# A running account for late matmuls, z in the head's gaps, and a lower bound moved to GpSimd: an adaLN block with Mamba and hyper-connections

## The chip, the core and the metric

The kernel runs on one core of one Trainium2 chip. Its time is device microseconds (us) of one execution; a run's figure is the median of several. Five engines work side by side, each through its own queue in order: TensorE (PE; its weight loads are shown as PEld), VectorE (DVE), ScalarE (ACT), GpSimd (POOL) and SyncE (SP). Loads are issued from SyncE's queue, most stores from ScalarE's. An instruction that waits holds up all that stands behind it on its engine.

## The reference

The input x is 4 x 512 x 1024 in float32. Six modulation rows per batch element come from one product, and the two gates are bounded below in size:

```python
mod = (_silu(L0_c) @ L0_wmod).reshape(L0_c.shape[0], 6, 1, -1)
sa, ca, ga, sb, cb, gb = (mod[:, 0], mod[:, 1], mod[:, 2], mod[:, 3], mod[:, 4], mod[:, 5])
ga = (2 * (ga >= 0) - 1) * jnp.maximum(jnp.abs(ga), 0.25)
gb = (2 * (gb >= 0) - 1) * jnp.maximum(jnp.abs(gb), 0.25)
h = _layernorm(x, axis=-1) * (1 + ca) + sa
x = x + ga * attn(h)
h = _layernorm(x, axis=-1) * (1 + cb) + sb
x = x + gb * ffn(h)
```

`attn` is a Mamba block: h is projected to x and z (2048 channels each); x goes through a causal convolution of four taps and a silu to xc; xc is projected to dt, B and C (64 + 16 + 16 columns), each normalized; dt is projected back to 2048 channels and through a softplus; a scan over time runs for each channel and each of 16 states, `h = exp(dt * A) * h + dt * B * xc`, and its outputs are summed over the states with C; D * xc is added, the result is multiplied by silu(z) and projected to 1024 columns. `ffn` mixes four streams of 256 columns with matrices that come from 50 Sinkhorn iterations on logits of the normalized h.

## The kernel before, in words

Time is cut into eight blocks of 256 rows (k = 0 to 7, two for each batch element), and the 2048 channels into four quads of 512 (q = 0 to 3).

**Head** (up to line 1191; a scheduler puts its instructions into order): the modulation products SA and CA, layernorm and transpose of block 0, then the eight x products of block 0 (`product_x`, matmuls pp at L613). Their finish on ScalarE, VectorE (L629, the taps) and GpSimd (L641) yields xc. Then `product_bc` (px, L694), whose finish normalizes, transposes (pe, L739) and stores B and C, then `stage_dt(0, 0)` (pd L771, softplus L782, u L803, the transposes pa L821 and the copies acc L826), then the two halves of z's first quad (`product_z`, pz L661; sgz, sz L673 to L678), then the transposes of block 1 (`norm(1)`, copies ht L583).

**Loop** (order written out by hand): 8 x 64 steps, one for each block, quad and state. A step g has two scans on VectorE (L1157), each over half of the quad's channels; four exponentials for step g + 1 on ScalarE (L1122); the scan's input w for step g + 2 on GpSimd (L1108), in one of three buffers; on TensorE eight transposes hq (L1133) of step g - 1 into two PSUM tiles; and on VectorE two sums of them into acc (L1143). Between these, a step has six ticks. At each tick, side tasks that wait for a gap in VectorE or for a due time are taken up, and `paced` (L369) hands out matmuls of the projections for later blocks. The products stand in one queue: x of the next block (pp), z (pz), the output projection of the block before (po, L842), B and C of the next block (px), and in block 0 the modulation products GA, CB, SB and GB (L425, L470). A unit of the queue is one 128-row matmul into 256 columns, two records in the trace. `go_on(budget)` (L338) takes units until the budget in columns is spent or the product at the front must wait. Each block has a planned rate (columns by ticks); what is behind the plan is `debt`, and transposes that other tasks put on TensorE are taken off it (`aside`). Weights come through three buffers; a load is issued when its product is among the first three of the queue.

The output products of block k - 1 wait for the last quad's y, which is ready some steps into block k. In the last block, three quarters of its own output product are taken early and wait for y of the third quad.

`product_rows` (L464) makes the rows CB, SB and GB in quarters of 4 x 256. For GB the finish takes a gap in VectorE and calls `away_from_zero` (L411): L412 to L415, four instructions. Then ScalarE's queue stores the quarter (L485).

**Tail**: the last quad is gated on VectorE (L911), transposed (py, L926) and multiplied (po), added to x and stored; the last two tiles go through layernorm to the FFN's logits; the Sinkhorn iterations of the other tiles run on VectorE meanwhile (L187 to L216), and the mixing products and sums end the kernel.

Of the kernel before, what the change touches and what calls it, by code (L numbers as in the profile page):

```python
# [12 lines left out]
ALU = mybir.AluOpType  # L13
# [7 lines left out]
TB = 256  # L21
# [10 lines left out]
STEPS = NQ * N  # L32
TICKS = 6
LAG, TAP_LAG, ACT_LAG, POOL_LAG, DMA_LAG = 2, 3, 5, 10, 12
MAKE_UP = 1.3
TURN = 64
E = R + 2 * N
NS, C = 4, 256
# [18 lines left out]
def adaln_block(  # L57
# [22 lines left out]
    vec, act, pool, pe = nc.vector, nc.scalar, nc.gpsimd, nc.tensor  # L80
# [32 lines left out]
    ab = const.tile([P, 2, NTT, NS], F32, name="ab")  # L113
# [154 lines left out]
    with ExitStack() as ph:  # L268
# [15 lines left out]
        clock = [0]  # L284

        def route(g):
            got = next(g, None)
            if got == "v":
                gaps.append(g)
            elif got is not None:  # L290
                waiting.append((clock[0] + max(got, 1), g))

        def spawn(g):
            route(g)

        def take(what, idle=1):
            while not free[what]:
                yield idle
            free[what] -= 1

        def give(what):
            free[what] += 1
# [10 lines left out]
        def due():  # L313
            for _ in range(len(waiting)):
                at, g = waiting.popleft()
                if at <= clock[0]:
                    route(g)
                else:
                    waiting.append((at, g))

        def drain():
            while gaps or waiting:
                while gaps:
                    route(gaps.popleft())
                clock[0] += 1
                due()
# [6 lines left out]
        def ahead():  # L333
            while loaded[0] < min(3, len(queue)):
                queue[loaded[0]][1]()
                loaded[0] += 1

        def go_on(budget):  # L338

            spent = 0  # L340
            while queue and spent < budget:
                ahead()
                got = next(queue[0][0], None)
                if got is None:
                    queue.popleft()
                    loaded[0] -= 1
                elif got == 0:
                    break
                else:
                    spent += got  # L350
            return spent

        def whole():

            while queue:
                if not go_on(1):
                    while gaps:
                        route(gaps.popleft())
                    clock[0] += 1
                    due()  # L360
            drain()
# [6 lines left out]

        def paced(parts):  # L369

            debt = 0.0
            for columns, ticks in parts:
                rate = columns / ticks
                for _ in range(ticks):
                    debt += rate - owed[0]
                    owed[0] = 0
                    if debt > 0:
                        debt -= go_on(min(debt, MAKE_UP * rate))
                    yield

        def wload(key, src, shape=(P, HC, TB)):
            def load_it():
                w = p1.tile(list(shape), F32, name="w_" + "_".join(map(str, key)), tag="wts", bufs=3)
                load(w, src)
                weights[key] = w

            return load_it
# [11 lines left out]
        def bank(name, shape):  # L399
            return ps_mm.tile(list(shape), F32, name=name, tag="mm")  # L400
# [10 lines left out]
        def away_from_zero(m, sg, ab):  # L411
            vec.tensor_scalar(sg, m, 0.0, 2.0, ALU.is_ge, ALU.mult)  # L412
            vec.tensor_scalar(ab, m, -1.0, 0.25, ALU.mult, ALU.max)
            vec.tensor_tensor(ab, ab, m, ALU.max)
            vec.scalar_tensor_tensor(m, sg, -1.0, ab, ALU.add, ALU.mult)  # L415
# [48 lines left out]
        def product_rows(kind, q):  # L464

            yield from take("mm", 0)
            w = weights.pop(("mod", kind, q))
            pm = bank(f"pmr_{kind}_{q}", (B, TB))
            for k in range(HC):
                pe.matmul(pm, sc[:, k, :], w[:, k, :], start=(k == 0), stop=(k == HC - 1))  # L470
                yield TB

            def finish():
                yield LAG
                yield from take("row")
                mr = p1.tile([B, 3, TB], F32, name=f"mr_{kind}_{q}", tag="row", bufs=5)
                m, sg, ab = mr[:, 0, :], mr[:, 1, :], mr[:, 2, :]
                act.activation(m, pm, AF.Copy, bias=1.0 if kind == CB else 0.0)
                give("mm")
                yield ACT_LAG  # L480
                if kind == GB:
                    yield "v"
                    away_from_zero(m, sg, ab)
                    yield LAG
                store(row_dram[kind][:, q * TB : (q + 1) * TB], m)  # L485
                give("row")

            spawn(finish())
# [17 lines left out]
        def load_constants():  # L506
            load(cw, conv_w)
            load(cb, conv_b)
            load(lnw, ln_w.partition_broadcast(P))
            load(dtb, dt_bias)  # L510
            load(dtw, dtproj_w)
            load(dpar, d_param)
            load(aneg, a_log)
            act.activation(aneg, aneg, AF.Exp)
            vec.tensor_scalar(aneg, aneg, -1.0, None, ALU.mult)
# [131 lines left out]
        def product_z(k, q, s):  # L647

            if s == 0:
                yield from until(("h", k), 0)  # L650
                m = NQ * k + q
                if m >= 2:
                    yield from until(("gate", m - 2), 0)
                szs[k, q] = p1.tile([P, TT, 2, 2 * P], F32, name=f"sz_{k}_{q}", tag="sz", bufs=2)
            sz = szs[k, q]
            yield from take("mm", 0)
            w = weights.pop(("z", k, q, s))
            pz = bank(f"pz_{k}_{q}_{s}", (P, TT, 2 * P))
            for t in range(TT):
                for h in range(HC):  # L660
                    pe.matmul(  # L661
                        pz[:, t, :], hts[k][:, h, PAD + t * P : PAD + (t + 1) * P], w[:, h, :],
                        start=(h == 0), stop=(h == HC - 1),
                    )
                    yield TB
            if s == 1:
                done.add(("z", k, q))

            def finish():
                yield LAG  # L670
                yield from take("sgz")
                sg = p1.tile([P, TT, 2 * P], F32, name=f"sgz_{k}_{q}_{s}", tag="sgz")
                act.activation(sg, pz, AF.Tanh, scale=0.5)  # L673
                act.copy(sz[:, :, s, :], pz)
                give("mm")
                act.activation(sg, sg, AF.Copy, scale=0.5, bias=0.5)  # L676
                yield ACT_LAG
                pool.tensor_tensor(sz[:, :, s, :], sz[:, :, s, :], sg, ALU.mult)  # L678
                give("sgz")
                if s == 1:  # L680
                    done.add(("sz", k, q))

            spawn(finish())
# [339 lines left out]
        def add_x(k, lo, hi):  # L1023
            for p in range(lo, hi):
                queue.append((product_x(k, p), wload(("x", k, p), in_w[p])))

        def add_z(k, q):
            for s in range(2):
                queue.append((product_z(k, q, s), wload(("z", k, q, s), in_w[NP + 2 * q + s])))

        def add_bc(k):
            queue.append((product_bc(k), wload(("bc", k), xproj_w, (P, DC, E))))
# [147 lines left out]
        whole()  # L1180
        load_constants()
        add_x(0, 0, NP)
        add_bc(0)
        whole()
        spawn(stage_dt(0, 0))
        drain()
        add_z(0, 0)
        whole()
        spawn(norm(1))
        drain()  # L1190
# [2 lines left out]
        with tc.manual_schedule():  # L1193
# [5 lines left out]
            for k in range(NBLK):  # L1199
# [9 lines left out]
                for s in range(STEPS):  # L1209
                    g = k * STEPS + s  # L1210
                    q, n = divmod(s, N)
# [31 lines left out]
    with ExitStack() as ph:  # L1243
# [12 lines left out]
        for i in range(NTT):  # L1256
# [5 lines left out]
            k, r = divmod(i, TT)  # L1262
# [164 lines left out]
```

## Time and profile before

| what | us or share |
|---|---|
| median of three runs | 2542.53 (2541.72 to 2544.48) |
| profiled execution: its time, its span | 2546.19, 2544.4 |
| mean granted clock of TensorE | 0.963 |
| head, up to the first scan | 128.3 |
| loop, first scan to the last sum | 128.3 to 2308.0 |
| tail | 2308 to 2544 |

Times in the trace are microseconds from the span's start. Busy shares say how full an engine is; a line of a group names the source line, engine and operation, the output and inputs with their sizes, how many there were, busy time and mean duration (ns), and the idle time of the engine ahead of them with what ended most of it. Most of the working below goes by single stretches: a timeline gives start, duration, engine, line and operation, with the idle time ahead of it in brackets.

### The profile page before, as it was taken

Reading aid. Unit: us, or ns where it says so; the run is one execution under the profiler, and the core shown is the slowest. Engines: PE = TensorE matmul, PEld = TensorE weight load, DVE = VectorE, ACT = ScalarE, POOL = GpSimd, SP = SyncE. Lnnn points to the kernel's source line nnn. Section 1 sums busy time; section 2 is a strip of 40 time slices with the busy share of each in tenths; the row PEclk is TensorE's granted clock in tenths of the full one; section 3 lists DMA queues with packets and bytes.
Section 4 is the critical chain, followed back from the end, with each engine's and each line's share of the span. In section 5 each row is a group of like instructions: output and inputs, shape, how many; then the busy total and the mean of one; then the engine's idle time right before and its main releaser. Section 6 shows DMA issues by size and latency. Waiting matters only on the chain.

```text
span 2544.4 us, 38522 instructions
## 1 busy us (share of the span) xinstructions
PE 2351.9 (92%) x13224; PEld 1969.1 (77%) x13224; DVE 2286.8 (90%) x3539; ACT 1701.3 (67%) x3775; POOL 1803.9 (71%) x1199
## 2 busy tenths in 40 slices
PE   8899989999999999999999999999999999885578
PEld 5766577888888887888788878887888877774567
DVE  2289999999899998999899999999999989979988
ACT  2366567676867686767777786768676767752466
POOL 0257568777967697778877796779676888872395
PEclk9899989999999999999999999999999999987689
DMA  7433423334423343334333433343333422323802
GB/s 262 144 134 133 150 96 133 108 120 150 142 101 123 125 162 112 114 134 151 110 131 108 154 133 108 127 143 141 111 114 110 161 100 100 116 92 102 315 18 116
DMA packets 74339, 330.98 MB, mean 130 GB/s; under 512 B 8496, under 2 KB 25312, under 8 KB 47456
## 3 DMA queue, kind: packets, MB, share of 16 engines
q1 hardware_dynamic: 62784, 311.56, 34.5%
q10 hardware_dynamic: 11360, 16.96, 1.8%
q8 instruction: 106, 1.74, 0.3%
q14 instruction: 89, 0.73, 0.1%
HBM read 303.14 MB, written 25.35 MB: 129 GB/s over the span
## 4 chain that ended last, share of the span: by engine, by line
PE 37%; DVE 24%; ACT 10%; POOL 7%; issue 6%; DMA 2%; POOLq 0%; SPq 0%; DVEq 0%; ACTq 0%
DVE w L1157 11%; PE po L842 9%; PE hq L1133 8%; PE pz L661 7%; PE pp L613 7%; DVE acc L1143 5%; ACT da L1122 4%; POOL w L1108 3%; DVE xc L629 2%; DMA xr<-x_dram 2%; PE oa L1336 1%; POOL hh L976 1%; ACT dv L782 1%; ACT L1122 1%; ACT L782 1%
## 5 line engine op out<-in xcount | busy, mean ns | idle before, releaser
L1108 POOL TENSOR_TENSOR w<-u,b 128x1024 f32<-128x1024 f32 x512 | 1209.1, 2363 | 478.5 <-PE hq L1133 359.4
L1122 ACT ACTIVATE da<-dv,aneg 128x255 f32<-128x255 f32 x2048 | 968.2, 476 | 568.9 <-DVE w L1157 512.5
L1157 DVE TENSOR_TENSOR_SCAN w<-da,w 128x512 f32<-128x512 f32 x1024 | 1203.6, 1207 | 66.4 <-ACT da L1122 32.7
L1143 DVE SCALAR_TENSOR_TENSOR acc<-hq,ss,acc 128x512 f32<-128x512 f32 x1024 | 723.5, 737 | 60.3 <-PE hq L1133 57.4
L1133 PE MATMUL hq<-ident,w 128*128 128x128 f32 x4096 | 634.3, 279 | 65.2 <-DVE acc L1143 62.1
L1133 PEld LDWEIGHTS hq<-ident,w 128*128 128x128 f32 x4096 | 500.9, 143 | 214.7 <-issue 62.9
L661 PE MATMUL pz<-w_z,ht 128*128 128x256 f32 x2048 | 513.0, 383 | 0.0
L613 PE MATMUL pp<-ht,w_x 128*128 128x259 f32 x2048 | 507.2, 382 | 2.1 <-ACT acc L826 1.1
L842 PE MATMUL po<-y,w_out 128*128 128x256 f32 x2048 | 497.1, 381 | 0.2 <-ACT y L933 0.2
L613 PEld LDWEIGHTS pp<-ht,w_x 128*128 128x128 f32 x2048 | 364.1, 190 | 48.2 <-issue 2.4
L842 PEld LDWEIGHTS po<-y,w_out 128*128 128x128 f32 x2048 | 368.9, 191 | 40.2 <-ACT y L933 0.5
L661 PEld LDWEIGHTS pz<-w_z,ht 128*128 128x128 f32 x2048 | 364.5, 193 | 34.4
L629 DVE SCALAR_TENSOR_TENSOR xc<-pp,cw,xc 128x256 f32<-128x256 f32 x384 | 181.1, 472 | 42.9 <-ACT xc L622 38.9
L641 POOL TENSOR_TENSOR xc<-xc,sx 128x1024 f32<-128x1024 f32 x32 | 75.5, 2361 | 43.1 <-ACT sx L639 42.8
L622 ACT ACTIVATE xc<-pp,cb,cw 128x256 f32<-128x256 f32 x128 | 71.2, 556 | 43.7 <-PE pp L613 43.1
L678 POOL TENSOR_TENSOR sz<-sz,sgz 128x512 f32<-128x512 f32 x64 | 81.7, 1276 | 6.8 <-ACT sgz L676 6.8
L694 PE MATMUL px<-w_bc,xc 128*128 128x96 f32 x512 | 74.8, 297 | 11.3 <-POOL xc L641 11.3
L694 PEld LDWEIGHTS px<-w_bc,xc 128*128 128x128 f32 x512 | 71.5, 215 | 13.0 <-POOL xc L641 12.7
L803 POOL TENSOR_TENSOR u<-dv,xc 128x1024 f32<-128x1024 f32 x32 | 75.5, 2360 | 5.9 <-ACT dv L782 5.9
L976 POOL TENSOR_TENSOR hh<-hh,mrow 128x1024 f32<-128x1024 f32 x32 | 75.5, 2363 | 1.4 <-ACT hh L540 1.4
L771 PE MATMUL pd<-et,dtw 64*128 64x256 f32 x256 | 73.7, 410 | 0.5 <-ACT et L744 0.5
L911 POOL TENSOR_TENSOR acc<-acc,sz 128x1024 f32<-128x1024 f32 x31 | 73.3, 2363 | 0.5
(155 smaller groups left out, 2116.3 us busy)
## 6 DMA issues: line engine op xcount, KB each, us to landing
w_x<-in_w_dram SPq DMA_DIRECT2D x64, 1024.0 KB, 4.8
w_z<-in_w_dram SPq DMA_DIRECT2D x64, 1024.0 KB, 6.1
w_out<-out_w_dram SPq DMA_DIRECT2D x56, 1024.0 KB, 4.8
w_mod<-wmod_dram SPq DMA_DIRECT2D x24, 1024.0 KB, 4.9
b<-bcd SPq DMA_DIRECT2D x32, 512.0 KB, 4.5
xt<-x_dram SPq DMA_DIRECT2D x16, 512.0 KB, 6.4
xr<-x_dram SPq DMA_DIRECT2D x32, 256.0 KB, 5.2
x<-xr ACTq DMA_DIRECT2D x32, 256.0 KB
```

The costliest lines, as they stand in the source:

```text
L613: pe.matmul(pp, w[:, h, j * P : (j + 1) * P], hts[k][:, h, :], start=(h == 0), stop=(h == HC - 1),)
L629: vec.scalar_tensor_tensor(xc[:, c, :], pp[:, tap : tap + TB], cw[:, i, tap : tap + 1], xc[:, c, :], ALU.mult, ALU.add,)
L661: pe.matmul(pz[:, t, :], hts[k][:, h, PAD + t * P : PAD + (t + 1) * P], w[:, h, :], start=(h == 0), stop=(h == HC - 1),)
L678: pool.tensor_tensor(sz[:, :, s, :], sz[:, :, s, :], sg, ALU.mult)
L694: pe.matmul(px[:, t, :], xcs[k, i // QC][:, i % QC, t * P : (t + 1) * P], xpw[:, i, :], start=(i == 0), stop=(i == DC - 1),)
L842: pe.matmul(po, w[:, d - lo, :], ys[k, d // QC][:, d % QC, :], start=(d == lo), stop=(d == hi - 1),)
L976: pool.tensor_tensor(hh, hh, row, op)
L1108: pool.tensor_tensor(w, us[k, q], bts[k, n // NG][:, n % NG, :].unsqueeze(1).to_broadcast([P, QC, TB]), ALU.mult,)
L1122: act.activation(das[s][:, j, 1:], dts[k, q][:, 2 * s + j, 1:], AF.Exp, scale=aneg[:, i, n : n + 1],)
L1133: pe.transpose(h[:, c * P : (c + 1) * P], ws[g][:, c, t * P : (t + 1) * P], ident)
L1143: vec.scalar_tensor_tensor(acc[:, t, :], hqs.pop((g, t)), cts[k][:, t, n : n + 1], acc[:, t, :], ALU.mult, ALU.add,)
L1157: vec.tensor_tensor_scan(h, das[s].rearrange(row), h, 0.0, ALU.mult, ALU.add)
```

## The change

Three edits:

```diff
-MAKE_UP = 1.3
+MAKE_UP = 1.2
...
-            debt = 0.0
+            debt, room = 0.0, 0.0
             for columns, ticks in parts:
                 rate = columns / ticks
                 for _ in range(ticks):
                     debt += rate - owed[0]
                     owed[0] = 0
-                    if debt > 0:
-                        debt -= go_on(min(debt, MAKE_UP * rate))
+                    room = min(room + MAKE_UP * rate, 1.5 * TB)
+                    if debt > 0 and room > 0:
+                        spent = go_on(min(debt, room))
+                        debt -= spent
+                        room -= spent
                     yield
```

Before, the limit held for each tick by itself: with a rate of some 308 columns, 1.3 times it is 401, and as `go_on` takes whole units of 256, a tick with enough debt took two. Now `room` carries the overdraft from tick to tick, so that late products come at 1.2 times the rate on average; at most 384 columns are saved up.

```diff
                 if kind == GB:
-                    yield "v"
-                    away_from_zero(m, sg, ab)
-                    yield LAG
+                    pool.tensor_scalar(sg, m, 0.0, 2.0, ALU.is_ge, ALU.mult)
+                    pool.tensor_scalar(sg, sg, -1.0, None, ALU.add)
+                    pool.tensor_tensor(ab, m, sg, ALU.mult)
+                    pool.tensor_scalar(ab, ab, 0.25, None, ALU.max)
+                    pool.tensor_tensor(m, sg, ab, ALU.mult)
+                    yield POOL_LAG
```

Four VectorE instructions a quarter become five on GpSimd, and the store comes ten ticks after they are issued (`POOL_LAG`) instead of two. GA keeps the old form.

```diff
-        def add_z(k, q):
-            for s in range(2):
+        def add_z(k, q, *halves):
+            for s in halves or range(2):
...
         add_x(0, 0, NP)
+        add_z(0, 0, 0)
         add_bc(0)
         whole()
         spawn(stage_dt(0, 0))
-        drain()
-        add_z(0, 0)
+        clock[0] += 1
+        due()
+        add_z(0, 0, 1)
         whole()
```

In the head, the first half of z's first quad now stands ahead of px, and the second half behind pd and ahead of pa. Its weights are loaded ahead of those of px. In the order of ScalarE, the second half's sgz and sz, the copies acc and the eight ht now come after the exponentials of steps 0 and 1 and ahead of those of step 2.

## The prediction

> **What bounds the kernel now.** I read the page first, its totals and its costliest groups:
>
> ```profile
> PE 2351.9 (92%) x13224; PEld 1969.1 (77%) x13224; DVE 2286.8 (90%) x3539; ACT 1701.3 (67%) x3775; POOL 1803.9 (71%) x1199
> ...
> L1108 POOL TENSOR_TENSOR w<-u,b 128x1024 f32<-128x1024 f32 x512 | 1209.1, 2363 | 478.5 <-PE hq L1133 359.4
> ...
> L1157 DVE TENSOR_TENSOR_SCAN w<-da,w 128x512 f32<-128x512 f32 x1024 | 1203.6, 1207 | 66.4 <-ACT da L1122 32.7
> L1143 DVE SCALAR_TENSOR_TENSOR acc<-hq,ss,acc 128x512 f32<-128x512 f32 x1024 | 723.5, 737 | 60.3 <-PE hq L1133 57.4
> ```
>
> Two engines are nearly full, and VectorE waits almost only for the transposes hq, which stand in TensorE's queue between the projections' matmuls. From the timeline of VectorE I took the starts of the 512 steps: a step is 3.55 us where VectorE does only its two scans and two sums. TensorE needs 0.43 us for each product unit (two records; 20 records of L842 take 4.48 us) and 0.87 us for a step's hq. So from seven units a step on TensorE is the slower: 7 x 0.43 + 0.87 = 3.9 us. VectorE's idle time is 10 to 13 us in each of blocks 1 to 6, 44 in block 0 and 28 in block 7; a better pace can win no more.
>
> Next, the head by the timeline and the granted clock in short windows (us; busy time of PE, PEld, DVE, ACT, POOL; clock; DMA):
>
> ```profile
> 102.00:106.00 4.00, 0.04 (x1) 0.04 (x1) 0.00 (x0) 2.68 (x6) 2.35 (x1) 0.97 0.24 102
> 106.00:107.00 1.00, 1.00 (x5) 1.00 (x6) 0.00 (x0) 0.00 (x0) 0.00 (x0) 0.50 0.00 0
> ...
> 112.00:113.00 1.00, 1.00 (x9) 1.00 (x9) 0.00 (x0) 0.00 (x0) 0.00 (x0) 0.72 0.00 0
> ```
>
> TensorE waits 4.48 us for the last xc, and then its clock is half for some 6.5 us: 40 records of px take 7.84 us, while the first 24 took 2.81.
>
> **The change, part by part.** *Head.* z's first half (64 records; 43 took 9.44 us in the warm stretch, so 32 per half and 7.0 us) now stands ahead of px, from 98.67 to 105.7 us; xc is ready at 105.9. All 64 records of px then run warm, 64 x 0.117 = 7.5 us, to 113.4 instead of 113.8. What follows (ss, pe, softplus, u, the first w) is a chain over other engines, and the first scan stays at about 128.0 (128.34). The other half follows pd at 122.2, at half clock until about 126, and ends near 131.1. Then come, on ScalarE in its new order, sgz and sz (1.7), two acc (1.1), eight ht (3.76 for eight) and only then the exponentials of step 2, near 137.9: the third scan starts at 138.9 instead of 142.89, 3.9 earlier, and TensorE's third hq at 141.25 instead of 146.30, 5.05 earlier. From there TensorE is the limit, so 5.0 us would remain. But TensorE is now empty for 2.2 us ahead of that hq. What such a gap costs, other gaps show:
>
> ```profile
> 2190.00:2192.00 2.00, 1.94 (x9) 1.35 (x8) 2.00 (x4) 0.95 (x2) 2.00 (x1) 1.00 0.17 70
> 2192.00:2194.00 2.00, 0.00 (x0) 0.00 (x0) 1.97 (x5) 0.95 (x2) 1.84 (x4) 1.00 0.00 0
> 2194.00:2196.00 2.00, 1.84 (x9) 1.59 (x10) 2.00 (x4) 0.17 (x1) 1.15 (x4) 0.67 0.00 0
> 2196.00:2198.00 2.00, 2.00 (x8) 1.64 (x7) 2.00 (x3) 1.74 (x4) 1.45 (x1) 0.50 0.00 0
> ```
>
> After gaps of 2.22 and 1.97 us the clock fell to half; after 1.93 and 1.54 it did not. The nearest row is 2.22, so I take the fall: 6.5 us at half lose 3.2, and **1.8 us** remain (ends 1.0 and 5.5). The Trainium skill ("TensorE: Matmul & The Clock Gate", HAM oscillation) warns only of gaps over some 3.4 us, and by it the head would give 5.0; the rows just shown speak against it.
>
> *The modulation row.* Sixteen VectorE instructions go. Two of the four quarters:
>
> ```profile
> 287.74 1.95 DVE L412 TENSOR_SCALAR mr<-mr 4x256 f32<-4x256 f32 x1
> 289.62 2.42 DVE L413 TENSOR_SCALAR mr<-mr 4x256 f32<-4x256 f32 x1
> 292.08 0.41 DVE L414 TENSOR_TENSOR mr<-mr 4x256 f32<-4x256 f32 x1
> 292.52 0.41 DVE L415 SCALAR_TENSOR_TENSOR mr<-mr 4x256 f32<-4x256 f32 x1
> ...
> 296.43 1.69 DVE L412 TENSOR_SCALAR mr<-mr 4x256 f32<-4x256 f32 x1
> 298.05 0.28 DVE L413 TENSOR_SCALAR mr<-mr 4x256 f32<-4x256 f32 x1
> ```
>
> L413 takes 2.42 us here and 0.28 elsewhere: it ends just after GpSimd's multiply at 289.51 (2.38 us) does. The six steps from 276.26 to 310.12 last 33.86 us, and TensorE's work in them (hq at 278.17 to 309.05, less 3.97 idle) is 26.9. With VectorE free TensorE sets them, so 7.0 us go. What is late next is GpSimd. It gets twenty instructions, none of which the trace has at this size. Two-input ones lie between 0.40 (128 elements) and 1.27 (512), about 0.7; one-input ones between 0.23 (2 elements) and 0.7 at most, and an affine select of 128 took 0.29: I take 0.45. A batch of five is 2.75 us (ends 2.1 and 3.65). In the new order GpSimd does between w_35 and w_39 four batches, one gate multiply (2.35) and four w. By the 284.89 row it has finished a w some 2.4 us before its scan. The first batch and the gate use that up (2.75 + 2.35 + 2.36 against 2.4 + 4.4), and each later batch with its w is 5.1 against a step of 4.4: w_39 is 2.5 us late. Behind these stand, on ScalarE, the row's stores, issued in order ahead of the next exponentials; they wait to about the same time as w does, so I count the 2.5 once. **4.5 us** remain (ends 0 and 7.5).
> By the Trainium skill ("GPSIMD Engine Reference", Elementwise) a two-input element costs about 2.6 cycles and a one-input one 1.03, so a batch is, as an estimate, 1.8 us, and all but 0.5 of the 7.0 would stay.
>
> *The account.* Before, a late product was made up with two units in every tick, up to 12 a step; now 8 or 9. In **blocks 1 to 6** the eight steps from the first po have 10, 12, 8, 7, 8, 7, 6, 3 units before and 8, 8, 9, 9, 8, 9, 7, 3 after: 61 each. TensorE's excess over VectorE runs up to about the same sum either way, and only its crest changes. I take 0.2 us a block, **1.2** (ends: 0.4 gained, or 0.45 lost where the first such step, at 4.4, falls short of VectorE's 4.85). **Block 7, start**: 10, 12, 9, 6, 4, ... become 6, 7, 7, 6, 7, 7, ...; VectorE's 3.8 us of waits (0.22, 2.31, 0.46, 0.79) shrink to about 2.4: **1.4**. **Block 0**: 2, 12, 8, 7, 6, 6 become 0, 4, 8, 7, 8, 8, so more is left where px comes: 0.5 lost. **Block 7, end**, the largest:
>
> ```profile
> 2270.78 2.33 DVE L1157 TENSOR_TENSOR_SCAN w<-da,w 128x512 f32<-128x512 f32 x2
> 2275.74 0.75 DVE L1143 SCALAR_TENSOR_TENSOR acc<-hq,ss,acc 128x512 f32<-128x512 f32 x1 [2.64 <-PE hq L1133]
> 2277.05 0.75 DVE L1143 SCALAR_TENSOR_TENSOR acc<-hq,ss,acc 128x512 f32<-128x512 f32 x1 [0.55 <-PE hq L1133]
> ```
>
> Before: 10, 12, 12, 12, 12 units, then 5 to 7. TensorE's five steps are 58 x 0.432 + 5 x 0.87 + 5.2 for the FFN's transposes and logits = 34.6; less 5 x 3.55 that is 16.9, and VectorE's waits sum to 16.4. After: 92 units in twelve steps, 39.7 + 10.4 + 5.2 - 42.6 = 12.8, less the same 0.5: 12.3, so 4.1 us go. Four units are left over; they come behind py (2309.37) and ahead of the last eight products, which end the chain to x1 and the last logits: 4 x 0.432 less the 0.24 that TensorE waits there anyway, 1.5 back. **2.6** remain (ends 0.5 and 4).
>
> Sum: 1.8 + 4.5 + 1.2 + 1.4 - 0.5 + 2.6 = 11.0 us. The profiled execution took 2546.19 (span 2544.4), 3.66 over the median of 2542.53: 2535.2 for it, and **2531.5** for a median.
>
> **The rivals.** *GpSimd becomes the bound* at the modulation row: a batch of 3.65 makes w_39 6 us late, and little of the 7.0 is left: -6.5, 2536. For it: GpSimd is 54% busy in these steps and the batches come one a step; against it: 0.29 for the select.
> *The pace wins nothing*: TensorE's work is only moved within a stretch, as in blocks 1 to 6, and the leftover costs 1.5: 1.8 + 4.5 - 1.5 = 4.8, 2537.7. Against it: the 3.54 us steps after the last burst show room.
> *The head's gap leaves the clock up* (the skill's rule, above): 5.0 instead of 1.8, 2528.
> *Slower*: in blocks 1 to 6 TensorE starves for 0.7 to 2.0 us in the two or three steps ahead of the first po. Before, ten and twelve units follow at once; now eight at 4.4 in a step of 4.85, so some 0.45 of idle time is added. If that tips the clock to half, as after 1.97 at 634, it costs 3.2 a block, six times, and 2531.5 becomes 2551. It decides from a gap of about 2 us; the clock of 0.98 to 0.99 in those blocks and starving steps of mostly 0.9 speak against it.
> That the change does nothing is out: the instruction orders differ in all the places named.
>
> **Chances.** Forecast (2525 to 2537) 0.50; GpSimd 0.17; no gain by pace 0.13; clock up 0.10; slower 0.10. A difference under 0.2% (5.1 us) can't be told from none here. Below 2537.4 lie nearly all of the first and the fourth, over half of the second and a little under half of the third: faster 0.73, same 0.16, slower 0.11. The range 2523 to 2543 leaves out the slower rival and the best of the rest.
>
> **What would show it.** px with no half clock and the first four sums near 135 us; the clock near 141 decides the head. L412 to L415 with four quarters gone from VectorE, and steps 33 to 38 near 4.4 to 5; waits of the scan for w there mean GpSimd. Steps of 4.2 to 5.2 at the loop's end instead of 5.9 to 8. The forecast is wrong if blocks 1 to 6 change in length by over 1 us each, or if the tail after the last sum grows by over 3.

## The result, and the profile after

The changed kernel takes **2535.88 us** (median of six runs, 2532.36 to 2538.91), the kernel before 2544.52 (six runs, 2541.72 to 2549.61): 8.6 us less, a ratio of 0.9965 with a 95% interval of 0.9953 to 0.9977. The prediction said 2531.5 and a range of 2523 to 2543. The profiled execution took 2536.24 us (span 2534.4), 10.0 less than that of before. The page of the changed kernel, its totals and the three groups that were shown of before:

```profile
PE 2342.8 (92%) x13224; PEld 1964.2 (78%) x13224; DVE 2280.1 (90%) x3523; ACT 1701.0 (67%) x3775; POOL 1820.1 (72%) x1219
...
L1114 POOL TENSOR_TENSOR w<-u,b 128x1024 f32<-128x1024 f32 x512 | 1208.7, 2362 | 454.1 <-PE hq L1139 309.0
...
L1163 DVE TENSOR_TENSOR_SCAN w<-da,w 128x512 f32<-128x512 f32 x1024 | 1202.0, 1205 | 70.0 <-ACT da L1128 31.4
L1149 DVE SCALAR_TENSOR_TENSOR acc<-hq,ss,acc 128x512 f32<-128x512 f32 x1024 | 724.2, 736 | 54.2 <-PE hq L1139 47.3
```

The work is the same (13224 matmul records; 16 instructions fewer on VectorE, 20 more on GpSimd), and the averages say almost nothing: the wait of the sums for hq falls by 10 us, that of the scans grows by 4. So the two timelines were laid side by side by the starts of the 512 steps ("the last sum" is the start of the last step's two sums):

| stretch | before | after | won | predicted |
|---|---|---|---|---|
| to the first scan | 128.34 | 126.88 | 1.5 | 0.3 (in the head's 1.8) |
| first scan to step 34 | 157.15 | 153.45 | 3.7 | 1.5 (the rest of it) |
| steps 34 to 40 (GB) | 33.80 | 36.29 | -2.5 | 4.5 |
| steps 40 to 64 | 107.80 | 107.24 | 0.6 | -0.5 |
| blocks 1 to 6 | 1616.35 | 1613.62 | 2.7 | 1.2 |
| block 7 to step 490 | 162.59 | 159.46 | 3.1 | 1.4 |
| step 490 to the last sum | 100.53 | 97.45 | 3.1 | 4.1 |
| behind the last sum | 237.84 | 240.01 | -2.2 | -1.5 |
| sum | 2544.4 | 2534.4 | 10.0 | 11.0 |

The two sums, 10.0 and 11.0, agree to 1 us, and hardly a row does. The biggest miss is GB's row: time was lost where the largest gain was expected.

**The head**, by the same windows as before (times; busy of PE, PEld, DVE, ACT, POOL; granted clock; DMA), and two around the disputed gap:

```profile
106.00:107.00 1.00, 1.00 (x11) 1.00 (x11) 0.00 (x0) 0.88 (x2) 0.05 (x1) 1.00 0.91 139
112.00:113.00 1.00, 0.35 (x4) 0.19 (x2) 0.24 (x1) 0.33 (x1) 0.00 (x0) 1.00 0.00 0
...
140.00:142.00 2.00, 0.79 (x6) 0.51 (x6) 2.00 (x4) 1.40 (x4) 1.83 (x1) 1.00 0.00 0
142.00:144.00 2.00, 2.00 (x12) 0.90 (x11) 2.00 (x3) 0.96 (x3) 0.92 (x1) 1.00 0.00 0
```

px runs at full clock, with 11 records in the slice in which it had 5. TensorE did wait for the third hq, for 2.46 us up to 141.21, but the clock stayed at 1.00.

**GB's row**, GpSimd's timeline (start, duration, engine, line, operation):

```profile
291.26 1.07 POOL L485 TENSOR_SCALAR mr<-mr 4x256 f32<-4x256 f32 x1
292.42 0.86 POOL L486 TENSOR_SCALAR mr<-mr 4x256 f32<-4x256 f32 x1
293.36 0.72 POOL L487 TENSOR_TENSOR mr<-mr 4x256 f32<-4x256 f32 x1
294.16 0.84 POOL L488 TENSOR_SCALAR mr<-mr 4x256 f32<-4x256 f32 x1
295.08 0.72 POOL L489 TENSOR_TENSOR mr<-mr 4x256 f32<-4x256 f32 x1
295.77 2.34 POOL L1114 TENSOR_TENSOR w<-u,b 128x1024 f32<-128x1024 f32 x1
298.09 1.07 POOL L485 TENSOR_SCALAR mr<-mr 4x256 f32<-4x256 f32 x1
```

A batch is 4.5 us, not 2.75, and a batch and one w take 6.83 us (291.26 to 298.09), without a break on GpSimd. That is the length of these steps: GpSimd sets them. VectorE's scans and ScalarE's copies show it; both wait for GpSimd, in VectorE's timeline

```profile
291.32 2.34 DVE L1163 TENSOR_TENSOR_SCAN w<-da,w 128x512 f32<-128x512 f32 x2 [2.15 <-POOL w L1114]
298.15 2.34 DVE L1163 TENSOR_TENSOR_SCAN w<-da,w 128x512 f32<-128x512 f32 x2 [3.19 <-POOL w L1114]
```

and in ScalarE's, where the row's store stands ahead of this copy and waits for the bound:

```profile
296.12 0.59 ACT L939 COPY y<-py 128x512 f32<-128x512 f32 x1 [6.80 <-POOL mr L489]
```

**The end of the loop.** The bursts are flatter, but seven units of po now stand right ahead of the last hq, and the last sum waits for it (VectorE):

```profile
2290.06 1.62 DVE L1149 SCALAR_TENSOR_TENSOR acc<-hq,ss,acc 128x512 f32<-128x512 f32 x2
2294.39 1.41 DVE L1149 SCALAR_TENSOR_TENSOR acc<-hq,ss,acc 128x512 f32<-128x512 f32 x2 [2.71 <-PE hq L1139]
```

Before, no product stood there, and the last sums hardly waited:

```profile
2306.56 1.41 DVE L1143 SCALAR_TENSOR_TENSOR acc<-hq,ss,acc 128x512 f32<-128x512 f32 x2 [0.15 <-PE hq L1133]
```

**The tail** has a wait that the prediction had not foreseen, on ScalarE:

```profile
2353.95 0.25 ACT L140 ACTIVATE kernels<-z 128x96 f32<-128x96 f32 x1 [8.24 <-DVE z L216]
...
2354.51 1.06 ACT L1003 COPY hft<-pft 128x512 f32<-128x512 f32 x2
```

The four units left over are taken one in each turn of the tail's loop, so everything behind them is emitted four turns later, and the Sinkhorn iterations, which are handed out by turns as well, come ahead of it. ScalarE's two copies of the last transposed tile now stand behind a renewal of the Sinkhorn kernels (L140), which waits 8.24 us for VectorE; TensorE's last logits wait behind the copies:

```profile
2347.49 1.95 PE L1000 MATMUL pft<-ident,hh 128*128 128x128 f32 x8
2355.14 3.61 PE L1010 MATMUL plg<-w_sb,hft 128*128 128x24 f32 x16 [5.70 <-ACT hft L1003]
```

In the kernel before these logits follow their transposes without a wait:

```profile
2357.98 1.95 PE L994 MATMUL pft<-ident,hh 128*128 128x128 f32 x8
2359.80 3.61 PE L1004 MATMUL plg<-w_sb,hft 128*128 128x24 f32 x16
```

### The profile page after: what moved, and what is told of

Same layout as the page of the kernel before. It is cut to its first block, busy times and chain, and to the rows that moved or that the text cites. A ratio compares the mean times of both kernels' runs of the same rounds, so it can differ in the third digit from the quotient of the medians.

```text
span 2534.4 us, 38524 instructions
## 1 busy us (share of the span) xinstructions
PE 2342.8 (92%) x13224; PEld 1964.2 (78%) x13224; DVE 2280.1 (90%) x3523; ACT 1701.0 (67%) x3775; POOL 1820.1 (72%) x1219
## 4 chain that ended last, share of the span: by engine, by line
PE 57%; DVE 22%; POOL 7%; ACT 7%; issue 5%; DMA 2%; POOLq 0%; DVEq 0%; SPq 0%; ACTq 0%
PE po L848 13%; PE pp L619 13%; PE hq L1139 12%; PE pz L667 9%; DVE w L1163 9%; DVE acc L1149 5%; POOL w L1114 4%; ACT da L1128 2%; DVE xc L635 2%; PE pm L428 2%; PE pd L777 2%; PE pmr L473 2%; PE oa L1344 1%; DMA xr<-x_dram 1%; POOL hh L982 1%
## 5 line engine op out<-in xcount | busy, mean ns | idle before, releaser
L700 PE MATMUL px<-w_bc,xc 128*128 128x96 f32 x512 | 68.0, 278 | 6.8 <-POOL xc L647 6.8
L700 PEld LDWEIGHTS px<-w_bc,xc 128*128 128x128 f32 x512 | 64.5, 197 | 8.4 <-POOL xc L647 8.1
```

The costliest lines, as they stand in the source:

```text
L700: pe.matmul(px[:, t, :], xcs[k, i // QC][:, i % QC, t * P : (t + 1) * P], xpw[:, i, :], start=(i == 0), stop=(i == DC - 1),)
```

## The experiments

A run's time varies by some 4 us to either side, as much as most of the terms. So each kernel's time is given with its ratio to the kernel before on the same chip, and the terms are read from its profile, stretch by stretch; kernels that share an order of instructions in a stretch are repetitions of that stretch.

| kernel | us, ratio (95%) | step 0 to 34 | 34 to 40 | blocks 1-6 | 448 to 490 | 490 to last sum | behind it |
|---|---|---|---|---|---|---|---|
| before | 2544.5, 1 | 157.15 | 33.80 | 1616.4 | 162.6 | 100.5 | 237.8 |
| changed | 2535.9, 0.9965 (0.9953-0.9977) | 153.45 | 36.29 | 1613.6 | 159.5 | 97.5 | 240.0 |
| e1 account only | 2535.0, 0.9965 (0.9952-0.9977) | 156.64 | 33.80 | 1610.4 | 160.1 | 97.3 | 239.4 |
| e2 head only | 2540.3, 0.9987 (0.9978-0.9996) | 153.76 | 33.83 | 1618.8 | 163.1 | 100.7 | 235.3 |
| e3 GB only | 2546.8, 1.0010 (1.0001-1.0019) | 156.61 | 36.28 | 1612.8 | 164.7 | 99.5 | 237.5 |
| e4 GB as before | 2533.6, 0.9965 (0.9953-0.9977) | 153.37 | 34.19 | 1610.6 | 159.4 | 97.5 | 240.1 |
| e5 GB as 128 x 32 | 2527.4, 0.9931 (0.9920-0.9943) | 153.20 | 26.94 | 1614.7 | 159.5 | 97.5 | 239.8 |
| e6 no bound on GB | 2526.0, 0.9930 (0.9916-0.9943) | 154.60 | 26.93 | 1611.1 | 159.3 | 97.3 | 239.4 |
| e7 five units more | 2533.5, 0.9957 (0.9945-0.9969) | 153.77 | 36.31 | 1610.5 | 159.5 | 99.2 | 237.9 |
| e8 e5 and e7 | 2527.3, 0.9933 (0.9921-0.9945) | 153.36 | 26.95 | 1614.3 | 159.3 | 99.5 | 237.8 |
| e9 units in the gap | 2528.6, 0.9943 (0.9929-0.9957) | 153.43 | 36.27 | 1613.2 | 159.5 | 97.6 | 236.2 |
| e10 e5 and e9 | 2523.4, 0.9925 (0.9913-0.9938) | 153.27 | 26.94 | 1611.6 | 159.3 | 97.5 | 235.9 |
| e11 128 x 32 on GpSimd | 2526.1, 0.9937 (0.9924-0.9949) | 153.29 | 26.95 | 1610.4 | 159.4 | 97.7 | 240.3 |
| e12 pace 1.1, units in gap | 2531.7, 0.9963 (0.9950-0.9975) | 154.74 | 36.30 | 1615.0 | 160.4 | 94.0 | 239.3 |

**e1, e2, e3: each of the three edits alone**, put on the kernel before (the diffs are those of the change).

> Only the account and the 1.2; the head and GB as before. Theory A (the scan starts of the two traces, read step by step): the account is worth what is left of the 10 us after the head's 5.1 and GB's -2.5, so some 7 us: 0.2 or 0.3 in block 0, 2.5 to 3 over blocks 1 to 6, 3 at the start of block 7, 2 to 3 at its end, and about 1.5 to 2 lost again behind the last sum. Rival (from the prediction: the account only moves work): within 2 us of before, and blocks 1 to 6 each as long as before to 0.2 us.

> Only z's first quad around px and dt. Theory A: 5 us faster, with TensorE's clock at full behind the gap of some 2.4 us near 141 us. Rival 1 (the prediction's): the clock falls to half there and 1.8 us remain. Rival 2: the 5 us are there up to step 30 but are waited away before the end of block 0, because some other thing (GB, or the products of block 0) sets the time; then the whole gains under 2.

> Only GB's lower bound on GpSimd; the old pace and head. Theory A: 2.5 us slower (1.5 to 4), since four batches of about 4.5 us make w late by more than VectorE gains; steps 35 to 38 at 6.6 to 6.9 us. Rival (the prediction's): 4.5 us faster, if the loss seen in the changed kernel comes from the pace of block 0 and not from GpSimd.

e1 takes 9.3 us off by the medians, where some 7 were expected: the account carries the change, and the rival (it only moves work) falls. In its profile blocks 1 to 6 are 6.0 us shorter; 2.5 to 3 were expected of them. e2 takes 4.1 off by the medians and 3.3 by the ratio, where 5 were expected. Its profile wins 3.4 us up to step 34 and gives 1.3 back in block 0, all in step 63 (4.88 us instead of 3.56), just after the clock had fallen to half at 417.38. The changed kernel has no fall there, and its step 63 keeps 3.56 us; so what e2 gave back goes with the clock, and the second rival, which has another engine or product set the time, is not borne out. e3 adds 2.5, and the interval leaves out a gain. Together these are -10.9, and the changed kernel has -8.6 with an interval of some 3 us to either side: within that noise the edits add up. e1 and e3 also correct the first table. Both have the old head, yet their first scan comes at 126.69 and 127.00, and that of e2, with the new one, at 127.52. The first scan comes at 126.7 to 128.3 in the three old heads and at 126.4 to 128.1 in the eleven new ones, so the 1.5 us ahead of it is chance, and the head is worth the 3.3 us behind it (156.6 to 157.2 against 153.2 to 153.8 in all but e6 and e12, of which below).

**e4: the changed kernel with GB's bound on VectorE again.**

> The changed kernel with GB's bound back on VectorE as before. Theory A: 2.5 us faster than the changed kernel, some 12.5 us under the kernel before; steps 34 to 40 take some 33 us instead of some 36. Rival: as slow as the changed kernel or slower, if the stalls around steps 35 to 38 come with the new pace or the new phase of block 0, whoever does the bound.

The six steps take 34.19 us instead of 36.29: 2.1 less, where 2.5 was expected. The whole, 0.9965, can't tell such a difference from none. The five kernels with four batches on GpSimd at the pace of 1.2 or 1.1, or the old one, all have 36.27 to 36.31 here, and the four with the bound on VectorE in quarters 33.80 to 34.19; so these steps depend on GB's form and hardly on the pace.

**e5 and e6: what GB costs at all.** e5 stores the quarters unbounded and treats the whole row once, in another shape:

```diff
-                if kind == GB:
-                    pool.tensor_scalar(sg, m, 0.0, 2.0, ALU.is_ge, ALU.mult)
...
                 store(row_dram[kind][:, q * TB : (q + 1) * TB], m)
                 give("row")
+                if kind == GB and q == 3:
+                    yield 10 * DMA_LAG
+                    flat = row_dram[GB].rearrange("b (p f) -> (b p) f", f=H * B // P)
+                    m = p1.tile([P, H * B // P], F32, name="gbm")
+                    load(m, flat)
+                    yield 2 * DMA_LAG
+                    yield "v"
...
+                    away_from_zero(m, sg, ab)
+                    yield DMA_LAG
+                    store(flat, m)
```

e6 leaves out the bound (the first part of this diff alone), so it does not compute the reference; it only shows what the steps take without it.

> The changed kernel, but GB's four quarters are stored unbounded, loaded again as one tile of 128 x 32 some 20 steps later, bounded there by VectorE's four instructions and stored back. Theory A (the shape 4 x 256 is what costs, on either engine): steps 34 to 40 take 27 us, as TensorE alone needs, instead of 36.3, and the four instructions take 0.2 us each; some 9 us faster than the changed kernel. Rival: something else holds these steps (the stores of rows on ScalarE, the products of CB, SB and GB), and they stay over 32 us; under 4 us faster.

> The changed kernel with GB's lower bound left out (the row is stored as it comes), so no engine does it. Theory A: steps 34 to 40 take 27 us, and this is the floor for them: GpSimd's bound costs 9 us in all, VectorE's 7. Rival (VectorE's form cost only its own wait): 30 us or more.

Both take 26.94 us for the six steps. So the bound on VectorE cost 6.9 us (33.80 less 26.93), the bound on GpSimd 9.35, and in the shape 128 x 32 nothing that these steps show. There the bound falls into step 60, which takes 6.45 us in e5 and 5.80 in e6: on VectorE it still costs 0.65 us. The four instructions of e5, some 25 steps later on VectorE:

```profile
402.29 0.28 DVE L415 TENSOR_SCALAR sg_gb<-gbm 128x32 f32<-128x32 f32 x1
402.48 0.17 DVE L416 TENSOR_SCALAR ab_gb<-gbm 128x32 f32<-128x32 f32 x1
402.68 2.22 DVE L417 TENSOR_TENSOR ab_gb<-ab_gb,gbm 128x32 f32<-128x32 f32 x1
404.94 0.33 DVE L418 SCALAR_TENSOR_TENSOR gbm<-sg_gb,ab_gb 128x32 f32<-128x32 f32 x1
```

Three of them are short, as expected. The third took 2.22 us, where its twin on GA took 0.19; it ends at 404.90, just behind GpSimd's multiply:

```profile
402.49 2.37 POOL L1119 TENSOR_TENSOR w<-u,b 128x1024 f32<-128x1024 f32 x1
```

It is the picture that the prediction showed for L413: here a small instruction that met GpSimd's big one took about as long as what was left of it. In e8, with the same form, it is the instruction ahead of this one that takes 2.39 us beside GpSimd's 2.35, and this one takes 0.34.

**e11: the same shape on GpSimd.** As e5, but with the change's five GpSimd instructions instead of `away_from_zero`.

> GB's bound on GpSimd as in the change, but on one tile of 128 x 32 that was stored and loaded again, instead of four times on 4 x 256. Theory A (the number of elements on a partition and the four batches in a row are what cost): five instructions of 0.2 to 0.5 us once, steps 34 to 40 in 27 us, and within 1 us of the same form on VectorE (2527.4). Rival: GpSimd's instructions keep 0.7 to 1.1 us whatever the shape, one batch of 4.5 us makes w late once, and it is 2 us or more slower than that form.

```profile
404.54 0.35 POOL L494 TENSOR_SCALAR sg_gb<-gbm 128x32 f32<-128x32 f32 x1
...
405.38 0.25 POOL L496 TENSOR_TENSOR ab_gb<-gbm,sg_gb 128x32 f32<-128x32 f32 x1
...
406.10 0.25 POOL L498 TENSOR_TENSOR gbm<-sg_gb,ab_gb 128x32 f32<-128x32 f32 x1
```

The five take 1.8 us from first to last, and the whole is as e5's (0.9937 against 0.9931). Step 60, in which they run, takes 5.79 us, as without a bound (5.80 in e6), and 6.45 to 6.65 with VectorE's form (e5, e8, e10). So it was the shape, 256 elements on each of 4 partitions four times over, and not the engine: the edit's idea is sound on 128 partitions. The place moved too, by some 25 steps, and no run moves the old shape there; but twenty instructions of 0.71 to 1.09 us became five of 0.25 to 0.35, whatever the place.

**e7 and e8: the leftover taken into the loop.**

```diff
-                columns = 8 * OC + 3 * ZC, 8 * OC * SPLIT // DC
+                columns = 8 * OC + 3 * ZC, 8 * OC * SPLIT // DC + 5 * TB
```

> The changed kernel; in the last block the plan for the late products holds five units more, so that the four units that were left over after the loop run in it. In the new order ScalarE's copies of the last transposed tile again come ahead of the renewal of the Sinkhorn kernels. Theory A (the tail after the last sum lost 3 us by the four units and by those copies waiting for VectorE): the tail goes from 240.0 back to 237 us or so, the loop's end is up to 1 us longer, and 2 us are won in all. Rival 1: only the units counted, the tail wins 1.5 and the loop gives it back: no change. Rival 2: the tail is set by the Sinkhorn iterations on VectorE, which begin with the last sum whatever TensorE does; the tail stays at 240.

> Both the 128 x 32 form of GB's bound and the five units more in the last block, on the changed kernel. Theory A: the two add, 11 us faster than the changed kernel, some 2525. Rival: one of the two is covered by other work; 8 us or less.

The tail goes from 240.0 to 237.9 and 237.8, so the second rival falls: the tail hangs on what TensorE and ScalarE are given there. The units and the order of ScalarE's copies change together, and no run changes the order alone. But the loop's end grows from 97.5 to 99.2 and 99.5, where Theory A had allowed 1. That is the four units, 1.7 us: they only change places. The whole wins the expected 2 us in e7 (0.9957 against 0.9965 of the changed kernel, with intervals that overlap) and nothing in e8 against e5 (0.9933 and 0.9931), so that e8 is some 8 us faster than the changed kernel, near its rival's 8 and not 11. Little or nothing is won.

**e9 and e10: the leftover put where TensorE idles.** Behind the last hq TensorE waits 2.42 us for VectorE's gate.

```diff
                 emit_sum(LAST - 1, t)
+            while go_on(TB):
+                pass
             spawn(gate_quad(NBLK - 1, NQ - 1))
```

> The changed kernel; the four units left over after the loop are put on TensorE right behind the last hq, ahead of py, where TensorE waits 2.42 us for VectorE's gate anyway, instead of behind py one by one. ScalarE's copies of the last transposed tile come ahead of the Sinkhorn renewal again. Theory A: the loop keeps its 97.4 us from step 490 to the last sum, and the tail goes from 240 to 237.5: 2.5 us faster than the changed kernel. Rival: the loop and the tail trade, as when the units ran in the loop, and less than 0.7 is won.

> Both: GB's bound in the form 128 x 32 on VectorE and the four units in the gap behind the last hq. Theory A: the two add, 9 + 2.5 = 11.5 us under the changed kernel, some 2524.5, the fastest so far. Rival: the tail's part is taken up elsewhere, and it is no faster than the 128 x 32 form alone (2527.4).

TensorE in e9:

```profile
2295.24 1.89 PE L848 MATMUL po<-y,w_out 128*128 128x256 f32 x8
2297.82 1.06 PE L932 MATMUL py<-ident,acc 128*128 128x128 f32 x8 [0.69 <-DVE acc L917]
2299.12 5.88 PE L848 MATMUL po<-y,w_out 128*128 128x256 f32 x26 [0.24 <-ACT y L939]
```

The eight records fill the gap, py comes 2.81 us after the last sum begins, as in all kernels but e12, and the loop's end stays at 97.6. The tail is 236.2, 3.8 less than in the changed kernel; 2.5 was expected. Part of the rest is the clock: 26 records of po take 5.88 us at full clock, and 7.57 in the profile of before, where the clock was at half for 3.4 us of them; e1 and e6, which have the leftover but ran at full clock here, have a tail 0.7 us shorter than the four that did not (239.4 against 240.1 on average). All three kernels with the filled gap (e9, e10, e12) ran at full clock behind the loop; of the eleven with an unfilled one e1, e2 and e6 did and eight did not, so that filling it keeps the clock up is likely, not shown. e10 has **the lowest median of the study**: 2523.39 us, 0.9925 (0.9913 to 0.9938), 18 us under the kernel before on its chip. Its interval overlaps those of e5, e6, e8, e9 and e11, so that it leads is read from the stretches.

**e12: the account at 1.1**, beside e9 (`MAKE_UP = 1.1`).

> As the kernel with the four units in the gap, but with 1.1 instead of 1.2 times the pace; twelve units are then left over at the end. Theory A (the account only moves work between steps: what the first eight steps of a block win, the next 24 lose in part): steps 0 to 8 of blocks 1 to 6 a little shorter, steps 8 to 32 longer, the sum within 2 us of 1612; from step 490 to the last sum about 94 us, and 2.5 to 3 us more in the tail; within 1.5 us in all. Rival (a lower crest is what pays): blocks 1 to 6 shorter by another 3 us or more.

Blocks 1 to 6 give 1615.0, so a still lower crest does not pay. The sums of steps 0 to 8 and 8 to 32 over the six blocks tell why: 218 and 591 us at the old pace (three profiles), 205 and 600 at 1.2 (ten profiles), 197 and 611 at 1.1. Of the 13 us that the first eight steps win from the old pace to 1.2, the next 24 give back 9; from there to 1.1 they give back 11, more than the 8 won. The end came out as worked out: 94.0 us in the loop, and py 2.6 us later behind twelve units. In all it is 3 us (by the medians) to 5 us (by the ratios) behind e9, more than the 1.5 expected.

## Where the prediction was right and where not

The total fell inside the range and the sign was right, but partly because errors cancelled: GB's row was forecast 7 us too good and block 7's end with the tail 2.8, the head, block 7's start and blocks 1 to 6 together 7 us too bad. That the total came out near is luck: the measured 2535.9 is the 2536 of the rival "GpSimd becomes the bound", and GpSimd did set those steps, but the rival kept the other terms of the forecast, and those were off as well. The repetitions above give each term better than two profiles do.

- **The head: 1.8 predicted, 3.3 measured.** The order, px at full clock and the third hq as the place where it is decided were right. What failed is the step "the nearest row is 2.22, so I take the fall": the gap came, 2.46 us and longer than that row, and in the changed kernel and eight more the clock did not fall. That the rival's 5.0 was not reached either has its cause ahead: the first scan does not come earlier, and the third hq starts 14.33 us after it, not 13.25. And the price of a fall was too high: in e6 and e12 the clock did fall, for 3.4 us instead of 6.5, and step 34 came 1.2 to 1.3 us later, not 3.2.
- **Why the gap was the wrong measure.** In all 14 profiles the changes of the clock lie whole multiples of 3.41 us apart; in the profile of before the falls at 634.80 and 2194.69, which the prediction went by, lie 149 and 606 such steps behind the rise at 126.22. And that profile has falls with no long gap at all: TensorE waited 0.96 us up to 1963.61 and 1.00 us up to 1965.85, and the clock fell at 1966.00. So idle time counts by windows of 3.41 us, not gap by gap. Eleven kernels have the same gap of 2.46 us ahead of the third hq, at another place of the window each. The most idle time that one window held was 1.24 to 1.71 us in nine of them, and the clock stayed; 1.84 and 2.00 in e12 and e6, and it fell. The windows ahead of the prediction's two falls held 1.97 and 2.22. A gap of 2.46 us can cost nothing or a window at half clock, by its phase. But no sharp limit comes out of this: over the loops of all 14 profiles, of the windows at full clock that held over 1.8 us of idle time 105 of 108 were followed by a fall, of those with 1.4 to 1.8 us 66 of 127, of those with less 19 of 8337, down to 0.52 us. What else counts stays open. In e6:

```profile
140.00:142.00 2.00, 1.74 (x10) 0.95 (x10) 2.00 (x4) 0.66 (x3) 0.89 (x1) 0.92 0.03 8
142.00:144.00 2.00, 2.00 (x6) 0.61 (x6) 2.00 (x3) 1.81 (x5) 1.68 (x1) 0.50 0.00 0
```

  The Trainium skill ("TensorE: Matmul & The Clock Gate", What's actually happening) has such a free-running window, of 3413 ns, and these traces agree to the hundredth. Its rule of gaps over 3.4 us (HAM oscillation), which the prediction weighed, does not hold here: windows with some 2 us of idle time were nearly always enough.
- **The modulation row: 4.5 predicted, -2.5 measured.** "7.0 us go" was right, 6.9 by e6. (The prediction's six steps from 276.26 are steps 32 to 38, the table's 34 to 40, where the batches fall; both lasted 33.8 to 33.9 us before and take 26.9 to 27.0 in e6.) What failed is the step "I take 0.45" for a one-input instruction: they take 0.84 to 1.09 us, and the two-input ones the 0.7 that was taken, so a batch is 4.5 us and not 2.75, above even the upper end of 3.65. With that, the prediction's own mechanism (each batch with its w against a step) gives what was seen: 6.83 us a step. (Its own figures for the delay add up to 2.8 us, not the 2.5 that it took: 0.7 for the first batch and 0.7 for each of three more.) The rival "GpSimd becomes the bound" had it right; its 6.5 us against the 7.0 fell short of the 9.4 measured. The estimate from the Trainium skill ("GPSIMD Engine Reference", Elementwise), 1.8 us a batch, was further off.
- **Block 0's rest**: -0.5 predicted; 107.8 to 109.1 in the old pace and 107.2 to 109.0 in the new say only that it is small. Most of the spread goes with the clock: e2, e4 and e11 take 1.2 to 1.3 us longer in step 63, just after a fall that before and the changed kernel do not have there.
- **Blocks 1 to 6: 1.2 predicted, about 3.9 measured** (1612.8 to 1618.8 in three profiles, 1610.4 to 1614.7 in ten). The mechanism was right, the same sum and a lower crest, but the crest was undervalued: 13 us of it go in the first eight steps, and TensorE takes back only 9. By its own sentence ("over 1 us each") this is not yet wrong, at 0.65 a block. The two groups overlap, and part of their spread goes with the clock, which is at half for 24 to 41 us of these blocks: at the same 30.7 us before has 1616.4 and e1, e6 and e11 1610.4 to 1611.1, at the same 34.1 us e2 has 1618.8 and e4 and e10 1610.6 and 1611.6. By these pairs of like clock the account is worth 5 to 8 us here. The slower rival, a clock that tips there, came only in part: the clock is at half for 24 to 34 us in the three old profiles and for 27 to 41 in the ten new ones, and no block grew by its 3.2 us.
- **Block 7's start: 1.4 predicted, 4.0 measured** (162.6 to 164.7 against 159.3 to 160.1). The size of the waits left was taken too high.
- **Block 7's end and the tail: 2.6 predicted, -0.2 measured.** The loop's end won 2.8 instead of 4.1, since the last seven units stand right ahead of the last hq (a wait of 2.71 us where before had 0.15, shown above). The tail lost 3.0 on average (235.3 to 237.8 in before, e2 and e3, 239.4 to 240.3 in the six with the leftover at 1.2) instead of 1.5: 2.0 to 2.9 where the clock fell just behind the loop, 4.0 where it did not. That is at the edge of the prediction's own sign of being wrong, "over 3". The step that failed is "four units are left over ... 1.5 back": it counted the units (1.0 to 1.4 us at the last transposes pr in most profiles, about as said) and not the turns of the loop that they take, which put ScalarE's copies behind the Sinkhorn renewal.

## What to carry to other kernels

Before work goes to another engine, ask for its shape: here the same bound cost 9.35 us on 4 partitions on GpSimd and 6.9 on VectorE, and on 128 partitions, at a later place, 0.65 us or a little more on VectorE and nothing that its step shows on GpSimd. When late work is paced more evenly, look at where it ends: what is left over changes the order of all that is emitted behind it, and belongs into a gap that exists anyway. Read a change stage by stage and from several profiles: a total that comes out right can hide a term with the wrong sign.

## What the runs showed of the hardware

- The clock of TensorE changes on a grid of 3.41 us. After windows of that length with over 1.8 us of idle time it fell 105 times of 108, after 1.4 to 1.8 us 66 times of 127, after less 19 times of 8337 (loops of 14 profiles). Two waits of 1 us in one window were enough, and one of 2.46 us across two windows mostly was not.
- Small GpSimd instructions, on 4 x 256 in five kernels and on 128 x 32 in e11: one-input 0.84 to 1.09 us and 0.30 to 0.35; two-input 0.71 to 0.72 and 0.25. The one-input form is the slower one here, against what the prediction had assumed.
- A VectorE instruction on 128 x 32 that takes 0.19 us on GA's row took 2.22 beside a GpSimd multiply of 2.37 (e5); its two neighbours ahead, which started before that multiply did, took 0.28 and 0.17. Scans did not stretch like that: in before, the 556 that ran at least four fifths of their time beside such a multiply took 1.21 us on average, and so did the 100 that met none.
